# Three edits to a two-layer mixer kernel: layer 0's last pair of chunks, unread matrix products in waits, and the order of one step in the tail

## The chip, the cores and the metric

The kernel runs on one core of a Trainium2 chip. The core has engines that work side by side, each on its own list of instructions, in order: TensorE (PE; its weight loads are shown apart as PEld), VectorE (DVE), ScalarE (ACT), GpSimd (POOL), and SyncE (SP), which issues DMA transfers. The engines wait for each other by semaphores. The metric is the device time of one execution in microseconds, lower is better. The "granted clock" is the share of full speed that TensorE got in a stretch: 1.00 is full, 0.50 half.

## The reference, cut to what matters

The input is an image of 64 x 64 positions with 96 channels. Two layers follow each other; each adds a mixer and an MLP to its input.

```python
# layer 0
x = x + mixer0(ln(x))     # in-projection, depthwise conv, silu, cumulative state sums in 4 directions,
                          # layer norm, times silu(z), out-projection 192 -> 96
t = t + mlp0(ln(t))
# layer 1
x = x + mixer1(ln(x))     # in-projection, dense 3x3 conv over 192 channels, silu,
                          # selective scan in 4 directions, times silu(z), out-projection
t = t + mlp1(ln(t))
```

with

```python
def _layernorm(x, g, b, eps=1e-05):
    m = jnp.mean(x, -1, keepdims=True)
    v = jnp.var(x, -1, keepdims=True)
    return (x - m) * jax.lax.rsqrt(v + eps) * g + b
...
def _qlinear(x, W, b):
    y = q_acc(jnp.einsum('bsk,nk->bsn', q_mul(x), q_mul(W)))
    return q_acc(y + q_mul(b))
```

The MLP is two such linear maps, 96 to 384 and back, with a relu between. `q_mul` rounds to a float of 5 exponent and 2 mantissa bits, `q_acc` to one of 5 and 10 bits; the kernel gets these roundings by writing through fp8 and fp16 tiles.

## The kernel before, in words

The 4096 positions ("tokens") are cut into 8 chunks of 512. The stream `res` stays on the chip, token by token (128 partitions, four tokens each), and products that contract over channels need the chunk turned, channels on partitions; so each norm is followed by four transposes on TensorE and a copy.

The program has these stages: front of layer 0 (to 131 us), back of layer 0 (`back0`, 134 to 255 us), convolution and projections of layer 1 (from 256 us, TensorE alone), the scans (about 490 to 1382 us, VectorE), the tail (1389 to 1461 us).

**The back of layer 0** treats two chunks at a time, in four steps s = 0 to 3, with pairs (0, 2), (1, 3), (4, 6), (5, 7). The loop is skewed: turn s does work of step s + 1 (`centred`, `variance`), of step s, and of step s - 1 (`to_layer1`, `keep_in_proj`). The parts:

- `centred` (L1068): mean over the 192 channels by a product with a constant matrix `mean`, subtracted on VectorE; squares on ScalarE; GpSimd multiplies by the gate.
- `variance` (L1088): sums of squares, three products into one small tile; a root on ScalarE; two small DMAs bring it to tokens; a reciprocal on VectorE gives `factor`. It is a generator: one product runs where `next` is called, the others between the MLP's up products.
- `gated_sums` (L1105): the out-projection, four f32 products for a pair, and copies `ot` on ScalarE.
- `gated_out` (L1118): for one chunk, four transposes, four VectorE operations that scale by `factor` and add to `res`, then the MLP's norm (`norm_chunk` L160, and a cast to bf16 on GpSimd).
- `mlp_turn`, `mlp_up`, `mlp_down` (L1984 to L2027): four transposes `tf`; three bf16 up products with rounding on ScalarE, VectorE and GpSimd; twelve fp8 down products; the sum with `res`. Then `norm_chunk` again, for layer 1.
- `to_layer1` (L1130): transposes `tr` of that norm, a copy `xt`, and a DMA store of it. `keep_in_proj` (L1138): layer 1's first projection, two f32 products of 512 columns for a chunk, each two passes, and their copies into a padded image (`in_proj`, L326; copies on L333). The convolution reads that image.

`keep` fixes the order of the marked instructions on their engine as written; the others are placed by a scheduler.

**The tail** (`tail` L1797) is a pipeline over the 8 chunks, written as a list of steps that each round goes through for chunks of different age: `new` is the youngest, then `mid`, `next_`, `old`, `done`. All its instructions keep the written order. `mixed` (new): out-projection `o` on TensorE (L1831), the sum into `res` (L1833), mean and centring on VectorE. `square` (new): ScalarE. `deviation` (mid): sum on VectorE (L1845), root on ScalarE (L1846). `normed` (mid): reciprocal (L1850) and product (L1852) on VectorE, cast on GpSimd (L1854). `turned` (next_): transposes on TensorE (L1860) and a copy. Then `up`, `rounded`, `relu`, `down`, `brought`, `added` and `finish` of the MLP. A round thus holds VectorE's instructions for `added`, `mixed`, `normed`, `relu` in that order, and those of TensorE for `turned`, `mixed`, `up`, `down`, `up`.

Of the kernel before, what the change touches and what calls it, by code (L numbers as in the profile page):

```python
# [28 lines left out]
F32 = mybir.dt.float32  # L29
# [10 lines left out]
P = 128  # L40
# [8 lines left out]
CH = 512  # L49
# [71 lines left out]
class Net:  # L121
# [897 lines left out]
    def back0(self):  # L1019

        tc = self.tc
        self.xn_d = self.scratch("xn1", [CD, L])
        with ExitStack() as ctx:
            self.tp = ctx.enter_context(tc.tile_pool(name="af0", bufs=3))
            self.lp = ctx.enter_context(tc.tile_pool(name="al0", bufs=2))  # L1030
            self.pa = ctx.enter_context(tc.tile_pool(name="ps_a0", bufs=3, space=PSUM))
            self.po = ctx.enter_context(tc.tile_pool(name="ps_o0", bufs=2, space=PSUM))
            self.ph = ctx.enter_context(tc.tile_pool(name="ps_h0", bufs=2, space=PSUM))
            self.pt = ctx.enter_context(tc.tile_pool(name="ps_t0", bufs=1, space=PSUM))
            self.w_in = self.w_in1
            n = NCH // 2
            self.sq, self.factor, self.xb, self.xn, self.xt, self.hid = {}, {}, {}, {}, {}, {}

            def chunks(s):
                c0 = s // 2 * 4 + s % 2  # L1040
                return (c0, c0 + 2) if 0 <= s < n else ()

            for s in range(-1, n + 1):
                if s + 1 < n:
                    self.centred(s + 1, chunks(s + 1))
                if 0 <= s < n:
                    self.gated_sums(s, chunks(s))
                for k in range(2):
                    for c in chunks(s - 1)[k : k + 1]:
                        self.to_layer1(c)  # L1050
                    for c in chunks(s)[k : k + 1]:
                        self.gated_out(c)
                for c in chunks(s - 1):
                    self.keep_in_proj(c)
                sums = self.variance(s + 1, chunks(s + 1)) if s + 1 < n else iter(())
                next(sums, None)
                for c in chunks(s):
                    self.mlp_turn(0, c)
                    self.mlp_up(0, c, lambda: next(sums, None))
                for _ in sums:  # L1060
                    pass
                for c in chunks(s):
                    self.mlp_down(0, c)
                    self.xn[c] = self.norm_chunk(self.lp, c, self.eps6, F32, f"c{c}")

    def keep(self, instruction):
        self.tc.keep_in_program_order(instruction)
# [740 lines left out]
    def tail(self, ctx, ph, y, out, parts, rest):  # L1808
# [55 lines left out]
        def up(c, m):  # L1864
            a = ph.tile([P, CH], F32, tag="hs", name=f"h1{c}{m}")
            keep(nc.tensor.matmul(a, w1[:, m * P : (m + 1) * P], xt[c], start=True, stop=True))
            hid[c, m] = a

        def rounded(c, m):
            h = tile3(f"h16{m}", c, [P, CH], F16)  # L1870
            keep(nc.scalar.copy(h, hid[c, m]))
            hid[c, m] = h

        def relu(c, m):
            h = hid[c, m]
            if m == 0:
                keep(nc.scalar.activation(h, h, AF.Relu, bias=b1[:, m : m + 1]))
            else:
                keep(nc.vector.tensor_scalar(h, h, b1[:, m : m + 1], 0.0, ALU.add, ALU.max))
            hid[c, m] = tile3(f"h8{m}", c, [P, CH], FP8)  # L1880
            keep(nc.gpsimd.tensor_copy(hid[c, m], h, saturate=False))  # L1881
# [23 lines left out]
        def pick(s):  # L1905
            return order[s] if 0 <= s < NCH else None

        for s in range(-3, NCH + 1):
            new, mid, next_, old, done = (pick(s + d) for d in (3, 2, 1, 0, -1))
            steps = [  # L1910
                (next_, turned),
                (mid, deviation),
                (done, added),
                (new, mixed),
                (next_, lambda c: (up(c, 0), rounded(c, 0), up(c, 1), rounded(c, 1))),
                (mid, normed),
                (done, finish),
                (next_, lambda c: relu(c, 1)),
                (old, down),
                (next_, lambda c: (up(c, 2), rounded(c, 2))),  # L1920
                (new, square),
                (next_, lambda c: (relu(c, 0), relu(c, 2))),
                (old, brought),
            ]
            before, after = rest.get(s + 3, ([], []))
            for f in before:
                f()
            for c, f in steps:
                if c is not None:
                    f(c)  # L1930
            for f in after:
                f()
# [177 lines left out]
```

## Time and profile before

| what | value |
|---|---|
| median of 4 runs | 1454.28 us |
| lowest and highest run | 1445.24 and 1458.40 us |
| profiled execution | 1462.73 us |
| its span (first to last instruction) | 1460.9 us |
| its mean granted clock | 0.845 |
| PE busy | 1165.8 us (80%) |
| DVE busy | 1154.8 us (79%) |
| ACT busy | 910.1 us (62%) |
| POOL busy | 785.4 us (54%) |

The profile is of one execution, and its times count from the start of its span. In a timeline's row stand the start, the time, the engine, the line, the operation, output and inputs with their shapes, how many were joined in the row, and in brackets how long the engine was idle before, with what released it. Buffer numbers are left out of names, so one name can be of several chunks. Ends of matrix products are modelled, so a busy TensorE isn't one at its peak. Other rows used here: the 20 opening products of the program ("warm", L376; f32, 128 x 128) take from 1.74 to 8.91 us.

### The profile page before, as it was taken

Reading aid. Unit: us, or ns where it says so; the run is one execution under the profiler, and the core shown is the slowest. Engines: PE = TensorE matmul, PEld = TensorE weight load, DVE = VectorE, ACT = ScalarE, POOL = GpSimd, SP = SyncE. Lnnn points to the kernel's source line nnn. Section 1 sums busy time; section 2 is a strip of 40 time slices with the busy share of each in tenths; the row PEclk is TensorE's granted clock in tenths of the full one; section 3 lists DMA queues with packets and bytes.
Section 4 is the critical chain, followed back from the end, with each engine's and each line's share of the span. In section 5 each row is a group of like instructions: output and inputs, shape, how many; then the busy total and the mean of one; then the engine's idle time right before and its main releaser. Section 6 shows DMA issues by size and latency. Waiting matters only on the chain. (4 is left out here: it accounts for less than half of the span.)

```text
span 1460.9 us, 12894 instructions
## 1 busy us (share of the span) xinstructions
PE 1165.8 (80%) x3976; PEld 472.3 (32%) x3976; DVE 1154.8 (79%) x887; ACT 910.1 (62%) x1099; POOL 785.4 (54%) x461
## 2 busy tenths in 40 slices
PE   7998776999991787777776777767778888899875
PEld 4532223333430222222222222222223333344343
DVE  6294675023059999999999999999999999999875
ACT  3355564035066677777777776777777777778444
POOL 2001331000006677688877877787878677885445
PEclk7799896999995888888888888888889898978855
DMA  2044000004248453645473456545465547442201
GB/s 64 11 149 100 12 12 22 15 18 110 70 141 256 172 169 112 223 140 171 139 241 115 148 184 195 165 142 183 166 186 156 161 137 252 142 132 86 73 0 44
DMA packets 68850, 183.19 MB, mean 125 GB/s; under 512 B 21488, under 2 KB 35460, under 8 KB 61956
## 3 DMA queue, kind: packets, MB, share of 16 engines
q1 hardware_dynamic: 67480, 182.00, 40.2%
q8 instruction: 33, 0.54, 0.2%
q10 hardware_dynamic: 1292, 0.28, 0.1%
q14 instruction: 45, 0.37, 0.1%
HBM read 155.98 MB, written 20.47 MB: 121 GB/s over the span
## 5 line engine op out<-in xcount | busy, mean ns | idle before, releaser
L1573 POOL TENSOR_TENSOR hss<-h1s,xws 128x1024 f32<-128x1024 f32 x96 | 224.5, 2375 | 135.5 <-PE hs L1581 135.5
L1557 ACT ACTIVATE da<-dt1s,a 128x1024 f32<-128x1024 f32 x168 | 187.9, 1118 | 139.8 <-DVE xws L1568 83.7
L1581 PE MATMUL hs<-hss,ident 128*128 128x512 f32 x376 | 216.3, 659 | 53.1 <-DMA x2s<-bc 32.8
L1568 DVE TENSOR_TENSOR_SCAN xws<-da,xws 128x1024 f32<-128x1024 f32 x96 | 224.1, 2335 | 10.4 <-DVE xws L1568 2.7
L1557 ACT ACTIVATE da<-dt0s,a 128x1024 f32<-128x1024 f32 x168 | 187.4, 1115 | 70.6 <-DVE xws L1568 52.3
L1581 PE MATMUL hs<-h0s,ident 128*128 128x512 f32 x376 | 203.4, 624 | 0.4 <-DVE h0s L1568 0.4
L1568 DVE TENSOR_TENSOR_SCAN h1s<-da,h1s,xws 128x1024 f32<-128x1024 f32 x72 | 169.2, 2350 | 11.0 <-ACT da L1557 2.3
L1581 PEld LDWEIGHTS hs<-hss,ident 128*128 128x128 f32 x376 | 70.6, 204 | 185.9 <-issue 81.8
L1396 POOL TENSOR_TENSOR dun<-u,dtn 128x512 f32<-128x512 f32 x4 | 5.9, 1479 | 197.2 <-DVE dtn L1293 107.6
L1581 PEld LDWEIGHTS hs<-h0s,ident 128*128 128x128 f32 x376 | 76.0, 202 | 100.6 <-issue 95.7
L1602 PE MATMUL acc<-hc2s,fold 128*32 128x512 f32 x128 | 47.5, 832 | 61.3 <-POOL hc2s L1591 58.2
L1602 PE MATMUL acc<-hc0s,fold 128*32 128x512 f32 x128 | 46.8, 819 | 52.8 <-POOL hc0s L1591 52.8
L1602 PE MATMUL acc<-hc1s,fold 128*32 128x512 f32 x128 | 45.5, 799 | 51.1 <-POOL hc1s L1591 51.1
L1541 POOL TENSOR_TENSOR x1s<-x1s,dus 128x1024 f32<-128x1024 f32 x32 | 75.0, 2362 | 8.8 <-DMA x1s<-bc 8.8
L1541 POOL TENSOR_TENSOR x2s<-x2s,dus 128x1024 f32<-128x1024 f32 x32 | 75.1, 2361 | 6.4 <-DMA c1s<-bc 6.4
L1568 DVE TENSOR_TENSOR_SCAN x0s<-da,x0s 128x1024 f32<-128x1024 f32 x32 | 74.7, 2335 | 4.3 <-ACT da L1557 1.9
L1568 DVE TENSOR_TENSOR_SCAN x1s<-da,x1s 128x1024 f32<-128x1024 f32 x32 | 74.7, 2335 | 3.7 <-ACT da L1557 1.2
L1568 DVE TENSOR_TENSOR_SCAN x2s<-da,x2s 128x1024 f32<-128x1024 f32 x32 | 74.7, 2335 | 3.2 <-ACT da L1557 0.6
L1581 PE MATMUL hs<-x0s,ident 128*128 128x512 f32 x128 | 67.4, 609 | 0.2 <-DVE x0s L1568 0.2
L1581 PE MATMUL hs<-x1s,ident 128*128 128x512 f32 x128 | 66.4, 601 | 0.0
L1541 POOL TENSOR_TENSOR x0s<-x0s,dus 128x1024 f32<-128x1024 f32 x28 | 65.7, 2360 | 0.0
L1253 PE MATMUL cv<-pad,cw 128*128 128x512 f32 x144 | 64.3, 598 | 0.0
(346 smaller groups left out, 2370.8 us busy)
## 6 DMA issues: line engine op xcount, KB each, us to landing
c0s<-bc SPq DMA_DIRECT2D x184, 128.0 KB, 2.6
c1s<-bc SPq DMA_DIRECT2D x184, 128.0 KB, 2.6
x2s<-bc SPq DMA_DIRECT2D x32, 512.0 KB, 5.1
x0s<-bc SPq DMA_DIRECT2D x28, 512.0 KB, 3.6
x1s<-bc SPq DMA_DIRECT2D x28, 512.0 KB, 6.5
dus<-du SPq DMA_DIRECT2D x20, 512.0 KB, 5.4
dt1s<-dt SPq DMA_DIRECT2D x40, 256.0 KB, 6.8
dt0s<-dt SPq DMA_DIRECT2D x40, 256.0 KB, 4.7
```

What stands on the lines that cost most here:

```text
L1253: keep(nc.tensor.matmul(t, cw[0][:, tap, 0:P], v, start=tap == 0, stop=False))
L1396: keep(nc.gpsimd.tensor_tensor(dun, u[1][:, m], dtn, ALU.mult))
L1541: keep(nc.gpsimd.tensor_tensor(x, x, du[:, part[j]], ALU.mult))
L1557: keep(nc.scalar.activation(das[i, s], dts[o][:, part[j]], AF.Exp, scale=self.a6[:, g, k : k + 1]))
L1568: keep(nc.vector.tensor_tensor_scan(to, da, x, start, ALU.mult, ALU.add))
L1573: keep(nc.gpsimd.tensor_tensor(cols(hs)[:, w, :], grid(h1)[:, w, :], grid(xw)[:, w, :], ALU.add))
L1581: keep(nc.tensor.matmul(t, self.ident, x[:, chunk(m)], start=x is hs, stop=x is xs[i % 3]))
L1602: keep(nc.tensor.matmul(to, self.fold4, src, start=k == 0, stop=k == NK - 1))
```

## The change

Three edits.

1. A method `awake(products)` puts that many f32 products of 128 x 128 (`mean` times the identity) on TensorE; they write a PSUM tile that nothing reads. It is called in `back0` in turn -1 with 4 (behind the first means, ahead of the first variance), in turn 0 with 6 (behind the first product of the next variance, ahead of the MLP's transposes), in the last turn of a step (s = 3) with 4, and in turn 4 with 10.
2. The last pair. `gated_sums` of step 3 moves up to step 2's end, between the down products of chunk 4 and those of chunk 6. In turn 3 both `gated_out` come first, then the four products, then `to_layer1` of chunk 4, its `keep_in_proj`, and `to_layer1` of chunk 6, whose `keep_in_proj` moves behind the first chunk's up products. In turn 4 each chunk's projection follows its own transposes, where before both transposes came first.
3. In the tail `normed` of `mid` moves from behind the first up products of `next_` to ahead of `mixed` of `new`. On VectorE the reciprocal and the product so come ahead of the residual sum of the younger chunk; the orders on the other engines stay.

```diff
             for s in range(-1, n + 1):
+                last = s == n - 1
                 if s + 1 < n:
                     self.centred(s + 1, chunks(s + 1))
-                if 0 <= s < n:
+                if 0 <= s < n and not last:
                     self.gated_sums(s, chunks(s))
-                for k in range(2):
-                    for c in chunks(s - 1)[k : k + 1]:
+                if s == -1:
+                    self.awake(4)
+                if last:
+                    for c in chunks(s):
+                        self.gated_out(c)
+                    self.awake(4)
+                    for c in chunks(s - 1):
                         self.to_layer1(c)
-                    for c in chunks(s)[k : k + 1]:
-                        self.gated_out(c)
-                for c in chunks(s - 1):
-                    self.keep_in_proj(c)
+                        if c == chunks(s - 1)[0]:
+                            self.keep_in_proj(c)
+                elif s == n:
+                    self.awake(10)
+                    for c in chunks(s - 1):
+                        self.to_layer1(c)
+                        self.keep_in_proj(c)
+                else:
+                    for k in range(2):
+                        for c in chunks(s - 1)[k : k + 1]:
+                            self.to_layer1(c)
+                        for c in chunks(s)[k : k + 1]:
+                            self.gated_out(c)
+                    for c in chunks(s - 1):
+                        self.keep_in_proj(c)
                 sums = self.variance(s + 1, chunks(s + 1)) if s + 1 < n else iter(())
                 next(sums, None)
+                if s == 0:
+                    self.awake(6)
                 for c in chunks(s):
                     self.mlp_turn(0, c)
                     self.mlp_up(0, c, lambda: next(sums, None))
+                    if last and c == chunks(s)[0]:
+                        self.keep_in_proj(chunks(s - 1)[1])
                 for _ in sums:
                     pass
                 for c in chunks(s):
+                    if s == n - 2 and c == chunks(s)[1]:
+                        self.gated_sums(n - 1, chunks(n - 1))
                     self.mlp_down(0, c)
                     self.xn[c] = self.norm_chunk(self.lp, c, self.eps6, F32, f"c{c}")
+
+    def awake(self, products):
+
+        t = self.pa.tile([P, CH], F32, tag="a", name="awake")
+        for _ in range(products):
+            self.keep(self.nc.tensor.matmul(t[:, 0:P], self.mean, self.ident, start=True, stop=True))
...
                 (done, added),
+                (mid, normed),
                 (new, mixed),
                 (next_, lambda c: (up(c, 0), rounded(c, 0), up(c, 1), rounded(c, 1))),
-                (mid, normed),
                 (done, finish),
```

## The prediction

> **What bounds the kernel now.** I read first the slices of the whole span.
>
> ```profile
> PE   7998776999991787777776777767778888899875
> DVE  6294675023059999999999999999999999999875
> PEclk7799896999995888888888888888889898978855
> ```
>
> One slice is 36.5 us. From slice 14 to slice 37 VectorE is at 9: the scans of layer 1, which the change doesn't touch. Ahead of them, in slices 7 to 11, TensorE is at 9: the dense convolution, which can't start before layer 0's back has delivered its last chunk. Behind them is the tail, with no engine at 9. So a microsecond taken from the back (134.4 to 255.3 us) moves the convolution, the scans and the end by as much, and the same is true of one taken from the tail (1389 to 1461). Section 4 of the page covers only the last microseconds and decides nothing here.
>
> Second, the table of busy times by stretch. After the stretch come its length, then PE, PEld, DVE, ACT, POOL, and the granted clock.
>
> ```profile
> 150.00:160.00 10.00, 4.79 (x20) 1.74 (x16) 6.71 (x20) 4.19 (x10) 3.96 (x5) 0.68 0.00 1
> 160.00:170.00 10.00, 8.20 (x39) 2.63 (x39) 2.99 (x7) 6.45 (x12) 3.57 (x6) 0.63 0.01 0
> 190.00:200.00 10.00, 7.96 (x46) 3.29 (x45) 8.33 (x19) 5.23 (x12) 3.31 (x4) 1.00 0.01 0
> 240.00:250.00 10.00, 3.90 (x21) 2.73 (x22) 7.08 (x15) 3.27 (x8) 1.06 (x2) 0.50 0.06 19
> 260.00:300.00 40.00, 40.00 (x186) 15.35 (x184) 1.41 (x2) 1.26 (x2) 0.00 (x0) 1.00 0.06 14
> ```
>
> No engine fills the back: it is a chain through all of them. In two places its TensorE work runs at half clock, around 160 and from 225 to 252.7 us. 260 to 300 shows the convolution: PE alone, full clock.
>
> Third, TensorE's timeline at those places (start, duration, engine, line, operation, count, idle before and its releaser).
>
> ```profile
> 202.82 3.63 PE L331 MATMUL in<-xt,w_in 96*128 96x512 f32 x8
> 225.55 6.92 PE L331 MATMUL in<-xt,w_in 96*128 96x512 f32 x8
> 246.75 1.06 PE L188 MATMUL tr<-ident,lnxnc 128*96 128x128 f32 x4 [4.38 <-DVE lnxnc L180]
> 249.37 5.23 PE L331 MATMUL in<-xt,w_in 96*128 96x512 f32 x8
> ```
>
> The same eight passes of layer 1's input projection cost 3.63 us in step 2, 6.92 in step 3 and 5.23 in step 4. Only the clock differs. The third row has 4.38 us of idle TensorE, waiting for the last norm.
>
> Fourth, the tail's timeline, one round.
>
> ```profile
> 1424.12 0.30 ACT L1846 ACTIVATE lnvt<-lnvt,columns 128x4 f32<-128x4 f32 x1
> 1425.39 0.56 DVE L1833 TENSOR_TENSOR res<-res,o 128x384 f32<-128x384 f32 x1 [0.93 <-PE o L1831]
> 1427.05 0.17 DVE L1850 RECIPROCAL lnrt<-lnvt 128x4 f32<-128x4 f32 x1
> 1427.32 0.56 DVE L1852 TENSOR_TENSOR lnxqt<-lnxct,lnrt 128x384 fp8e5<-128x384 f32 x1
> 1428.01 0.51 POOL L1854 CAST xbt<-lnxqt 128x384 bf16<-128x384 fp8e5 x1 [2.51 <-DVE lnxqt L1852]
> 1428.57 0.66 PE L1860 MATMUL tf<-identb,xbt 128*96 128x128 bf16 x4 [0.86 <-POOL xbt L1854]
> ```
>
> The root of the older chunk is done at 1424.42, but its reciprocal stands in VectorE's queue behind a residual sum that waits for TensorE, so it runs at 1427.05. Through it TensorE, which has the sum's product behind the transposes, waits 0.86 us: a loop.
>
> [...] in the back the clock changes at 140.0, 153.7, 167.3, 225.3, 232.2, 235.6 and 252.7 us, all multiples of 3.41 us apart within 0.05. [...] the window 150.25 to 153.66 had TensorE busy 1.85 us of 3.41, and the clock fell. [...] the window 221.93 to 225.34 has 1.82 us busy, all transposes, and the clock fell behind it. [...]
>
> **The change part by part.**
>
> *Price of an added product.* The 20 opening products of the program (f32, 128x128, two passes each: 40 passes) take 7.17 us: passes start 0.21 us apart until 6.9 us, where the clock rises, and 0.11 apart after it. So a product costs 0.43 us at half clock, 0.22 at full; 4, 6, 10 cost 1.7, 2.6, 4.3 or 0.9, 1.3, 2.2.
>
> *Four ahead of the first step.* TensorE waits 1.54 us before 141.71, at full clock; 0.9 fits. Cost nothing, gain nothing; if that cover went, 0.9.
>
> *Six ahead of step 0's turn.* TensorE waits 2.98 us for GpSimd's cast until 157.99, at half clock; 2.6 fits by 0.4. [...] The MLP of step 0 (first transpose to last product) takes 11.58 us, from 157.99 to 169.57; in steps 1 and 2, at full clock, 9.52. So the clock is worth 2.06 us here. Both ends: 0 (the clock rises at 167.3 as now) to 2.06. I take half, 1.0.
>
> *Last pair's sums earlier, projections split, four products.* Work is the same plus four products (0.9 to 1.7 us, some 0.5 to 1 on the path, since TensorE's idle time of 1.76 us ahead of 222.04 is filled by the moved transposes). The moved gated sums (3.1 us of TensorE) lie between step 2's down products, which wait 1.12 us for GpSimd; their two copies on ScalarE (0.58 each) then stand ahead of the copy of chunk 6's down product there, and GpSimd's cast of chunk 7's norm comes behind two casts of hidden tiles. SyncE's stores of the transposed chunks go along with the transposes; nothing in the back waits for them (cost nothing; one store, 3 us, if something did). The four products need one of three PSUM tiles that the projections use, free at that point; the same holds for the ten. I laid all instructions from step 2's down products to the last copy into the padded image in the new order, each engine in order, with the trace's durations. With the clock as it was granted before: 0 us gained. At full clock before and after: 0.9 us lost. At half clock throughout: 1.2 lost. So the reordering in itself brings nothing (0 to −1.2); its use is that transposes no longer stand alone for a window. New order at full clock against before as granted: 5.1 us gained, with the next edit's share in it.
>
> *Ten in front of the last two chunks.* They lie in the 4.38 us gap. At full clock 2.2, at half 4.3: it just fits. With 1.0 us of down products just ahead, TensorE is then busy about 5.3 us, and holds a whole window of 3.41 in some 55% of positions. What it is worth: transposes 1.06 to 0.61 twice, projections 5.23 to 3.63, less what VectorE's norm at 248.2 gates: up to 1.8 us, within the 5.1.
>
> *Sum for the back.* The windows stand where they happen to stand against the program, so the clock's gain is between 0 and 5.1 + 2.1 = 7.2. I take half of 5.1 and half of 2.1, 3.5 together, less 0.5 for the products that lie on the path: **3.0 us**.
>
> *The tail.* Reciprocal and product, 0.17 + 0.56 us, leave the loop: after them the cast could end at about 1425.7, and TensorE's transposes follow its own last product, at about 1427.7 instead of 1428.57. That is up to 0.86 us in each of four rounds, 3.4. Against it: after the swap VectorE waits for ScalarE's root in the early rounds, where the reciprocal stood under the sum (0.4 us once, its wait in the last round: 1443.72 + 0.30 to 1444.06); one round is held by gating of an earlier quarter (1.56 us before 1430.79); and the end is a chain of copies on ScalarE and casts on GpSimd, with 2.7 us waits that don't shrink. Both ends: −0.4 to +2.5. I take **1.5 us**. Nothing moves on TensorE, ScalarE, GpSimd or SyncE there.
>
> Profiled execution: 1462.73 us, of which 1460.9 span; 4.5 less is about 1458.2. It lies 8.45 us (0.6%) above the median of the runs, 1454.28, which themselves spread over 13 us. The difference carries over to the median: **1449.8**.
>
> **The rivals.**
> 1. *Clock lifted only in parts*, the forecast: 1449.8, chance 0.50.
> 2. *Clock full from step 0 on* to the end of the back (7.2) and the tail's best (2.5): 1444.6, chance 0.17. For it: steps 1 and 2 stay full with TensorE 75 to 80% busy. Against: windows with half of it already fell.
> 3. *The clock doesn't rise*, the products only fill waits: back 0, tail 1.5: 1452.8, chance 0.20. For it: the window 225.34 to 228.76 was full by the records and the clock rose only after the next. Then the change doesn't do what it says.
> 4. *Slower: the unread products run at half clock on the path.* TensorE can't pass them: ten at 4.3 us started 0.5 late, plus four at 1.7, plus the reordering's 1.2, with 2.6 us of six. On the path 0.5 + 1.2 + 0.5 + 1.2 = 3.4 us; and the tail gains nothing as VectorE stands before the root. 1457.7, chance 0.13. It decides from the point where the ten products end after the norm's product for the next to last chunk (246.6 us in the trace of before).
>
> **How the numbers follow.** About 1%, 14.5 us, is what a measurement of this kernel can tell from no change (four runs spread 13). Every case lies within it. The scatter of a median adds some 3 us to each case. The range 1443 to 1457.5 holds the first three with that scatter, and leaves out the lower part of case 2 and half of case 4. Faster by over 1%: 0.05, from case 2 and scatter; slower by over 1%: 0.03; within: 0.92.
>
> **What would show it.** Granted clock over 0.75 in the stretches that answer to 150 to 170 and 225 to 250; the projections in steps 3 and 4 near 3.6 us rather than 6.9 and 5.2; the start of the convolution (255.8) near 252.8; tail rounds from sum to sum below 5.98 us. Wrong if unread products delay the transposes behind them, if the reciprocal shows waits for the root of over 0.5 us in every round, or if the scans' length changes.

## The result, and the profile after

The changed kernel takes 1445.07 us (median of 39 runs, 1438.28 to 1454.53). The kernel before, run beside it, takes 1450.96 us (60 runs, 1443.99 to 1462.66). The ratio is 0.9955, with a 95% interval of 0.9939 to 0.9971: by the ratio 6.5 us faster, at least 4.2 and at most 8.9. Forecast were 4.5 us less, to 1449.8, from a median of four runs that lay 3.3 us above that of sixty.

The profiled execution of the changed kernel has a span of 1443.3 us, 17.6 less than the one of before. That is far more than 6.5, so the first question to the two traces is where the 17.6 lie. I cut both at the same instructions: the first product with `mean` (start of the back), the first `spread4p` (start of the convolution), the first out-projection `o` (start of the tail), the last instruction. "Half" is the time at half clock in the stage, the program's opening left out.

| us | front (half) | back (half) | convolution, scans | tail | span |
|---|---|---|---|---|---|
| before | 134.4 (39) | 121.1 (43) | 1133.9 | 71.6 | 1460.9 |
| changed | 124.9 (14) | 116.8 (27) | 1131.8 | 69.8 | 1443.3 |
| difference | -9.5 | -4.3 | -2.0 | -1.7 | -17.6 |

The largest difference is in the front, whose code is the same in both. The experiments deal with it; the back and the tail sum to 6.0.

The 2.0 us in the scans, whose code is the same too, aren't chance. VectorE's timeline at one place of the scans, before, and below it changed:

```profile
574.19 2.29 DVE L1568 TENSOR_TENSOR_SCAN xws<-da,xws 128x1024 f32<-128x1024 f32 x1
576.94 7.25 DVE L1568 TENSOR_TENSOR_SCAN xws<-da,xws 128x1024 f32<-128x1024 f32 x3 [0.46 <-DVE xws L1568]
```

```profile
560.47 9.65 DVE L1597 TENSOR_TENSOR_SCAN xws<-da,xws 128x1024 f32<-128x1024 f32 x4
```

Before, VectorE is idle for 0.46 us ahead of the second scan; in the changed kernel the same four scans follow each other. From the start of the first to that of the second it takes 2.75 us before and 2.39 changed. This is so at six places, every 64 scans: 2.1 us. All four kernels below with the old order in the back (before, tail_only, awake_only, front_hold) have 2.75 at all six, and all ten with the new order 2.39 or 2.40, with unread products or without. VectorE's instructions and their order are the same. So this gain goes with the second edit, whose code stands far from it. Why the idle time is there is open: the trace names VectorE's own scan before, which had ended at 576.48.

The slices of the span, after:

```profile
PE   7998778999981776787776777677779888899875
DVE  6494683033169999999999999999999999999876
PEclk8999997999995889888888888888889899987855
```

The scans fill VectorE as before. The clock's row differs in the first slices (7799 before, 8999 now): that is the front.

Busy times by stretch of the changed kernel (length, PE, PEld, DVE, ACT, POOL, granted clock, DMA share, GB/s); its back lies at 124.9 to 241.7 us:

```profile
140.00:150.00 10.00, 7.26 (x32) 3.78 (x32) 6.19 (x19) 4.73 (x11) 3.34 (x4) 0.83 0.00 1
150.00:160.00 10.00, 6.96 (x39) 3.20 (x38) 5.86 (x13) 5.60 (x11) 3.94 (x6) 0.83 0.01 0
220.00:230.00 10.00, 7.65 (x37) 4.06 (x36) 5.14 (x8) 4.83 (x10) 4.47 (x7) 0.50 0.01 0
230.00:240.00 10.00, 8.66 (x35) 6.28 (x34) 5.51 (x12) 3.64 (x9) 0.00 (x0) 0.76 0.12 32
```

Step 0's MLP (147 to 157) now has 0.83 where it had 0.63 to 0.68, and the last chunks (230 to 240) 0.76 where they had 0.50. The last MLP (220 to 230) is still at half clock.

TensorE's timeline in the last two turns:

```profile
211.05 1.98 PE L331 MATMUL in<-xt,w_in 96*128 96x512 f32 x4 [0.67 <-ACT xt L189]
214.02 0.61 PE L188 MATMUL tr<-ident,lnxnc 128*96 128x128 f32 x4 [0.99 <-DVE lnxnc L180]
216.63 0.42 PE L188 MATMUL tf<-identb,xb 128*96 128x128 bf16 x4 [2.00 <-POOL xb L2010]
219.42 3.62 PE L331 MATMUL in<-xt,w_in 96*128 96x512 f32 x4
229.50 4.60 PE L1093 MATMUL awake<-ident,mean 128*128 128x128 f32 x20
234.08 0.95 PE L188 MATMUL tr<-ident,lnxnc 128*96 128x128 f32 x4
235.71 1.98 PE L331 MATMUL in<-xt,w_in 96*128 96x512 f32 x4 [0.67 <-ACT xt L189]
238.80 1.98 PE L331 MATMUL in<-xt,w_in 96*128 96x512 f32 x4 [0.67 <-ACT xt L189]
```

Four passes cost 1.98 us at full clock and 3.62 at half. The clock falls at 217.7, behind 3.41 us in which TensorE had 0.73 us of transposes and otherwise waited, 2.0 us of it in one piece. It is back at 234.8, 17.06 us or five times 3.41 later. In this trace too, all changes of the clock lie multiples of 3.41 us apart; "window" is used below for such a stretch, with its edges where the clock's changes in the same trace put them. The ten products take 4.60 us, and the transposes follow without a wait: they start 4.66 us after the start of the last down product, exactly as before, where TensorE stood idle for 4.38 us. (Below, stretches "from the last down product" count from its start.)

The tail, one of the changed kernel's later rounds:

```profile
1403.15 0.18 DVE L1879 RECIPROCAL lnrt<-lnvt 128x4 f32<-128x4 f32 x1 [1.57 <-ACT lnvt L1875]
1403.43 0.56 DVE L1881 TENSOR_TENSOR lnxqt<-lnxct,lnrt 128x384 fp8e5<-128x384 f32 x1
1404.13 0.51 POOL L1883 CAST xbt<-lnxqt 128x384 bf16<-128x384 fp8e5 x1 [2.07 <-DVE lnxqt L1881]
1404.46 0.55 DVE L1862 TENSOR_TENSOR res<-res,o 128x384 f32<-128x384 f32 x1 [0.46 <-PE o L1860]
1406.57 0.63 PE L1889 MATMUL tf<-identb,xbt 128*96 128x128 bf16 x4
```

The product comes before the residual sum, though its reciprocal waited 1.57 us for ScalarE's root, the cast is done at 1404.64, and the transposes at 1406.57 wait for nothing. From out-projection to out-projection this round takes 4.89 us; the round in its place took 5.98.

### The profile page after: what moved, and what is told of

It is laid out like the page before. It is cut to its first block, busy times and chain, and to the rows that moved or that the text cites. A ratio compares the mean times of both kernels' runs of the same rounds, so it can differ in the third digit from the quotient of the medians.

```text
span 1443.3 us, 12990 instructions
## 1 busy us (share of the span) xinstructions
PE 1154.0 (80%) x4024; PEld 472.0 (33%) x4024; DVE 1156.2 (80%) x887; ACT 909.9 (63%) x1099; POOL 785.1 (54%) x461
## 5 line engine op out<-in xcount | busy, mean ns | idle before, releaser
L1602 POOL TENSOR_TENSOR hss<-h1s,xws 128x1024 f32<-128x1024 f32 x96 | 224.6, 2377 | 134.4 <-PE hs L1610 134.4
L1610 PE MATMUL hs<-h0s,ident 128*128 128x512 f32 x376 | 199.6, 613 | 0.8 <-DVE h0s L1597 0.8
```

The lines of the kernel that those rows point to most:

```text
L1602: keep(nc.gpsimd.tensor_tensor(cols(hs)[:, w, :], grid(h1)[:, w, :], grid(xw)[:, w, :], ALU.add))
L1610: keep(nc.tensor.matmul(t, self.ident, x[:, chunk(m)], start=x is hs, stop=x is xs[i % 3]))
```

## The experiments

All stages, cut as above, with mean and standard deviation of the runs and the ratio to the kernel before that ran beside them:

| kernel | front (half) | back (half) | conv., scans | tail | mean (s.d., runs) | ratio (95%) |
|---|---|---|---|---|---|---|
| before | 134.4 (39) | 121.1 (43) | 1133.9 | 71.6 | 1452.1 (5.2, 60) | 1 |
| changed | 124.9 (14) | 116.8 (27) | 1131.8 | 69.8 | 1445.6 (5.1, 39) | 0.9955 (0.9939 to 0.9971) |
| tail_only | 119.1 (0) | 121.7 (38) | 1133.3 | 70.2 | 1451.5 (5.4, 20) | 0.9991 (0.9963 to 1.0018) |
| back_only | 126.1 (17) | 116.8 (27) | 1133.0 | 71.2 | 1448.1 (4.5, 20) | 0.9967 (0.9943 to 0.9990) |
| order_only | 127.8 (21) | 120.0 (38) | 1133.0 | 71.2 | 1452.7 (4.4, 12) | 1.0010 (0.9979 to 1.0041) |
| awake_only | 130.5 (27) | 120.3 (34) | 1131.4 | 71.6 | 1449.3 (5.6, 12) | 0.9969 (0.9930 to 1.0007) |
| doubled | 121.5 (7) | 120.0 (24) | 1129.1 | 71.2 | 1446.2 (3.2, 20) | 0.9954 (0.9935 to 0.9973) |
| no_ten | 119.1 (0) | 120.7 (35) | 1135.5 | 71.2 | 1453.7 (4.9, 20) | 1.0010 (0.9988 to 1.0032) |
| hold | 121.6 (7) | 114.3 (17) | 1132.8 | 70.2 | 1443.8 (4.3, 20) | 0.9937 (0.9918 to 0.9956) |
| hold_late | 133.4 (35) | 115.4 (19) | 1132.7 | 69.2 | 1442.9 (5.3, 17) | 0.9941 (0.9917 to 0.9965) |
| front_hold | 118.9 (2) | 124.1 (50) | 1133.9 | 71.6 | 1448.0 (2.1, 22) | 0.9962 (0.9943 to 0.9981) |
| all_hold | 119.2 (2) | 115.2 (19) | 1132.6 | 69.2 | 1438.1 (1.3, 7) | 0.9898 (0.9863 to 0.9933) |
| tail_awake | 119.2 (1) | 116.7 (20) | 1132.2 | 77.3 | 1445.9 (1.9, 20) | 0.9954 (0.9935 to 0.9972) |
| change_front | 118.9 (2) | 117.2 (26) | 1130.7 | 69.8 | 1439.3 (1.8, 6) | 0.9912 (0.9881 to 0.9943) |

### The change taken apart: tail_only and back_only

```diff
 # tail_only: the kernel before, and only
+                (mid, normed),
                 (new, mixed),
...
-                (mid, normed),
```

> The tail's edit alone. My theory (reciprocal and product leave the loop between TensorE and VectorE): the tail, from its first out-projection to the end, takes 69.8 us as in the changed kernel and not 71.6; rounds 5 and 7 take 4.9 instead of 6.0; the back stays at 117 to 123, wherever the clock's windows fall; total 1.7 us less, ratio 0.9988. Rival (the tail was only shorter by a different granted clock): tail 71.6, ratio 1.000.

By time it can't be told from no change (0.9991, 1 within the interval). By the trace it can: the tail takes 70.2 us, and 71.2 to 71.6 in all seven kernels with the old order of tail and without further edits there. Rounds 5 and 7 take 4.89 and 4.86 us. The half-clock time in the tail is 65.6 of 70.2 us, where before has 68.2 of 71.6, so the gain isn't the clock's.

`back_only` is the changed kernel with the tail's step `normed` back in its old place.

> The back's edits alone (last pair and unread products), tail as before. My theory: back 114 to 119 us against 121 before, tail 71.6, ratio 0.9967 (4.8 us less). Rival (most of the gain is the tail's or chance): back 120 or more, ratio 0.999 or more.

The back takes 116.8, the tail 71.2, the ratio is 0.9967: as expected. The two parts add up, to 0.9958 against 0.9955 for the whole.

### Order or clock: order_only and awake_only

```diff
 # order_only: back_only without its four calls
-                    self.awake(4)
...
-                    self.awake(10)
...
-                if s == 0:
-                    self.awake(6)
```

> Only the last pair's new order, without any unread product, tail as before. My theory (the order gains nothing by itself, only the clock does): step 3 and 4 together, from step 2's last down product to the convolution, stay within 1.2 us of before when the clock is granted alike; ratio 0.999 to 1.001. Rival (the order is what gains, as the projections no longer stand in one block ahead of the MLP's transposes): back 117 us, ratio 0.997.

From step 1's last down product to the convolution order_only takes 62.7 us, and the kernels with the old order 61.9 (before), 62.6 (tail_only) and 65.0 (front_hold, where the clock fell once more in between). The changed kernel takes 59.7. The ratio, 1.0010 (0.9979 to 1.0041), shows no gain, though the 2.1 us of the scans, which this kernel has as well, would fit into its interval. That the back is 1.1 shorter than before's lies ahead of the last pair, in code that this kernel doesn't change. So in the back the order by itself gains nothing, as I had reckoned. back_only differs from it in the products alone, and ran beside it: 116.8 against 120.0 us in the back, 27 against 38 of them at half clock, and means of 1448.1 against 1452.7 us. This is the plainest sign that the products, by the clock, are what gains.

```diff
 # awake_only: the kernel before, with the products in the same waits
+                if s == -1:
+                    self.awake(4)
+                if s == n:
+                    self.awake(10)
                 for k in range(2):
+                    if s == n - 1 and k == 0:
+                        self.awake(4)
                     for c in chunks(s - 1)[k : k + 1]:
                         self.to_layer1(c)
...
                 next(sums, None)
+                if s == 0:
+                    self.awake(6)
...
```

> Only the unread products (4, 6, 4, 10, in the same turns and waits), order and tail as before. My theory (the clock gains): step 0's MLP 9.6 us instead of 11.4, last down product to convolution 12 instead of 13.4, half-clock time in the back 20 to 30 us instead of 43; back 117 to 119, ratio 0.997 to 0.998. Rival (unread products on the path): back 122 to 124, ratio 1.001.

Half a miss. From the last down product to the convolution it takes 11.2 us, against 13.4 before: the ten work in the old order too. But step 0's MLP, from its first transpose, took 11.1 us, as the clock was at half from 154.7 to 161.5, in the middle of it. And in step 3 the clock was at half ahead of the four products and again behind them (16.3 us from step 2's last down product to step 3's transposes, against 15.0 before; front_hold, without any products there, has 16.4). Back 120.3. The ratio, 0.9969 with 1 in the interval, tells little.

### How much the ten are worth, and what twice as many cost: no_ten and doubled

`no_ten` is back_only without the call with 10.

> Back's edits without the ten products ahead of the last two chunks, tail as before. My theory (the ten lift the clock for the last transposes and projections): from step 3's last down product to the convolution 14.0 to 14.6 us instead of 12.1; back 118.8 to 119.3; ratio 0.998. Rival (the ten only fill the wait): 12.1 to 12.5 there, back 117.

TensorE's timeline of no_ten at the end of the back:

```profile
228.06 1.06 PE L188 MATMUL tr<-ident,lnxnc 128*96 128x128 f32 x4 [4.38 <-DVE lnxnc L180]
229.79 3.78 PE L331 MATMUL in<-xt,w_in 96*128 96x512 f32 x4 [0.67 <-ACT xt L189]
235.10 3.78 PE L331 MATMUL in<-xt,w_in 96*128 96x512 f32 x4 [0.67 <-ACT xt L189]
```

The 4.38 us wait is back, and every pass behind it is at half clock: 16.4 us from the last down product to the convolution, where back_only has 12.1, more even than the 14.0 to 14.6 that I expected. How much more differed with the place of the windows: order_only, which lacks the ten too, has 14.6, and there the clock rose 3.6 us ahead of the convolution, and in no_ten only 5.6 us into it. So in no_ten the convolution begins at half clock and takes 2.7 us more to the first scan (196.7 against 194.0). Ratio 1.0010: without the ten, no gain is left that the runs show.

```diff
 # doubled: back_only with
-                    self.awake(4)
+                    self.awake(8)
...
-                    self.awake(4)
+                    self.awake(8)
...
-                    self.awake(10)
+                    self.awake(20)
...
-                    self.awake(6)
+                    self.awake(12)
```

> Back's edits with twice the unread products (8, 12, 8, 20), tail as before. In the changed kernel's trace the ten end just when the norm's product for the next transposes comes (both waits from the last down product to the transposes are 4.66 us). If a product costs 0.43 us at half clock, ten more put about 4.3 us on the path ahead of the last two chunks when the clock is half, and 2.2 when it is full; six more 1.3 to 2.6 less what is left of step 0's wait (0.5): back 120 to 124 us against 116.8 with the single number, ratio to before 0.999 to 1.002. Rival (more products hold the clock at full, so that the projections and the transposes win it back): back 114 to 117, ratio 0.995 to 0.997.

```profile
227.84 6.62 PE L1093 MATMUL awake<-ident,mean 128*128 128x128 f32 x40
234.29 0.60 PE L188 MATMUL tr<-ident,lnxnc 128*96 128x128 f32 x4
```

TensorE's timeline: the twenty take 6.62 us, half of them at full clock, and the transposes come 6.5 us after the last down product instead of 4.7. The stretch to step 0's transposes, with the eight and the twelve in it, takes 0.8 more, the one to step 3's transposes 1.3 more. In the profile the back takes 120.0 us, 3.3 more than with the single number, as my theory had it: from the point where the wait is full, each product is on the path. The ratio is the rival's, though: 0.9954, where I expected 0.999 or more and back_only has 0.9967 (the intervals overlap). So the runs don't show that twice as many are slower; only the trace does. In the profile the convolution and the scans took 1129.1 us, 4 less than back_only's. Those stages have the same code in both, and range from 1129.1 to 1135.5 over all kernels. Of that range no_ten's 2.7 us and the 2.1 that go with the back's order are located; doubled has the latter too. 2.0 of its 4 lie between the last scan and the tail (5.5 us against 7.5), as in awake_only; why is open.

### Two waits that were left: hold and hold_late

```diff
 # hold: the changed kernel with
...
                     for c in chunks(s - 1):
                         self.to_layer1(c)
+                    for c in chunks(s - 1):
                         self.keep_in_proj(c)
...
                 if s == 0:
                     self.awake(6)
+                if last:
+                    self.awake(8)
```

> The changed kernel with two more edits in the back: eight unread products in TensorE's 2.0 us wait ahead of the last pair's first MLP transposes, where the changed kernel's clock falls (217.7 us), and turn 4 in the old order (both transposes, then both projections). My theory: the clock doesn't fall in the last turn, so from step 2's last down product to step 3's last is 20.5 us instead of 23.0; the last stretch to the convolution 11.2 instead of 12.2; back 113 to 114, tail 69.8, ratio 0.993. Rival (the window is decided by more than that wait, and the products delay the cast's readers): 23 to 24 us there, back 116, ratio 0.995.

TensorE's timeline of hold, where the changed kernel had its clock fall:

```profile
211.22 1.95 PE L1096 MATMUL awake<-ident,mean 128*128 128x128 f32 x16
213.39 0.42 PE L188 MATMUL tf<-identb,xb 128*96 128x128 bf16 x4 [0.22 <-POOL xb L2013]
215.81 1.88 PE L331 MATMUL in<-xt,w_in 96*128 96x512 f32 x4
```

The eight fit into the wait, with 0.22 us left of it. The clock stays at full until 221.6. Step 2's last down product to step 3's last takes 21.5 us (23.0), the last stretch 11.2 (12.2), the back 114.3, ratio 0.9937; the interval overlaps the changed kernel's, so that the runs don't separate the two.

```diff
 # hold_late: hold, with
-                (mid, normed),
+                (None if s == -2 else mid, normed),
                 (new, mixed),
                 (next_, ...),
+                (mid if s == -2 else None, normed),
```

> As hold, with the tail's new order left out in its second round alone, where the norm's product is held by GpSimd's long product (1.85 us instead of 0.56) and holds the residual sum behind it. My theory: the tail's second round takes 6.6 us instead of 8.3, and the tail 68.5 instead of 69.8, ratio 0.992. Rival (a later round is held by a gate of its own and takes the gain back): tail 69.8, with a longer third or fourth round.

What it is about is the changed kernel's second round in the tail (timeline):

```profile
1379.93 2.34 POOL L1620 TENSOR_TENSOR hc1s<-hc1s,dus 128x1024 f32<-128x1024 f32 x1 [3.31 <-PE o L1860]
1380.63 0.18 DVE L1879 RECIPROCAL lnrt<-lnvt 128x4 f32<-128x4 f32 x1 [0.36 <-ACT lnvt L1875]
1380.84 1.85 DVE L1881 TENSOR_TENSOR lnxqt<-lnxct,lnrt 128x384 fp8e5<-128x384 f32 x1
1382.61 0.54 DVE L1862 TENSOR_TENSOR res<-res,o 128x384 f32<-128x384 f32 x1
```

The norm's product takes 1.85 us instead of 0.56, and ends 0.42 us behind GpSimd's product; the residual sum behind it, whose operands have been ready, comes late. In the old order this round took 6.55 us, in the new one 8.28. But the round ahead of it was shorter, 4.20 against 4.97, and it is so in awake_only and doubled too, which have the old order: the two rounds have to be summed. Together they took 11.5 before and 12.5 changed, 1.0 more. In hold_late they take 11.5 again, and 12.5 in hold. The tail follows: 69.2 us in hold_late and 70.2 in hold. (In the changed kernel, with 69.8, the end comes 23.5 us behind the last out-projection, in hold 23.9, though the code of the tail is the same.) That is half a miss, as I expected 68.5 for the tail, and the ratio (0.9941) doesn't separate it from hold.

### The front: front_hold, all_hold, change_front

The front has one code in all kernels and took 119 to 134 us, by its time at half clock. In eight of the first ten profiles the clock fell at 17 to 20 us and came back only at 24 to 55. TensorE's timeline of before, and below it of no_ten, one of the two where it didn't fall:

```profile
17.30 1.06 PE L409 MATMUL tr<-ident,lnxna 128*96 128x128 f32 x4 [1.98 <-DVE lnxna L405]
```

```profile
17.47 0.61 PE L409 MATMUL tr<-ident,lnxna 128*96 128x128 f32 x4 [2.16 <-DVE lnxna L405]
```

Both have the wait of 2 us; what differs in the traces is how the windows lie over it. In before, an edge between two windows is at 17.1: the window that ends there has TensorE busy for 1.61 of 3.41 us, with products, not transposes. In no_ten the edge is at 16.7 and divides the wait, and the windows on both sides are busy for 1.98 and 1.93 us. In the other eight it was alike: in tail_only, with 1.98 and 2.09, the clock stayed at full, and in seven it fell behind windows with 0.75 to 1.82 us.

```diff
 # front_hold: the kernel before, with
+            if i == 3:
+                warm = pm.tile([P, CH], F32, tag="m", name="warm3")
+                for _ in range(8):
+                    keep(nc.tensor.matmul(warm[:, 0:P], self.ident, self.ident, start=True, stop=True))
             if mid is not None:
```

> The kernel before, with eight unread products in one wait of the front, before the transposes of chunk 2 (TensorE waits 2.0 to 2.2 us there for VectorE's norm, and in eight of ten profiles the clock fell just after it, at 17 to 20 us, and stayed at half until 24 to 55 us). My theory (the scatter of the runs is this one drop: the front takes 119.1 us where it doesn't happen and 121 to 134 where it does): front 119 to 120 us, half-clock time in it 0 besides the opening, ratio 0.994 to 0.996, and the runs lie closer together than the 18 us of the kernel before. Rival (the scatter is in the scans): front as before on average, 126, ratio 0.999 to 1.001, same scatter.

```profile
15.13 1.95 PE L394 MATMUL warm<-ident 128*128 128x128 f32 x16
17.30 0.61 PE L413 MATMUL tr<-ident,lnxna 128*96 128x128 f32 x4 [0.22 <-DVE lnxna L409]
```

The front takes 118.9 us, the clock stays at full but for 2 us, the ratio is 0.9962, and the standard deviation of the runs falls from 5.1 to 2.1 us. So most of the scatter of the kernel before is this one wait. The profiled execution of before, with 134.4 us in the front, was a bad draw: the mean of the first ten profiles is 125.8.

`all_hold` has hold_late's edits and front_hold's.

> The changed kernel with all that the runs point to: eight products in the front's wait, eight in the wait of the last pair, old order in turn 4, and the tail's old order in its second round. If the parts add: front 119.5, back 114.3, tail 69.2, against 126 (mean of the profiles), 121 and 71.4 of before: 15.8 us less, ratio 0.989. Rival (the front's clock and the back's are tied by the same windows, so that one gain takes from the other): 0.992 or more.

1438.18 us median, ratio 0.9898 where 0.989 was expected if the parts add, standard deviation 1.3: the best of all, faster than both the kernel before and the changed one. The rival's 0.992 still lies within the interval (0.9863 to 0.9933).

`change_front` is the changed kernel with front_hold's lines.

> The changed kernel with the same eight products in the front's wait as front_hold, so that the change can be measured without the front's scatter: front_hold has a mean of 1447.97 us and a standard deviation of 2.1. If the change is worth what the stages of the profiles sum to (back 5.5, tail 1.3), the mean is 1441.2, ratio to the kernel before 0.992, standard deviation about 2. If only the predicted 4.5 are there: 1443.5. Rival (part of the measured 6.5 us is the front's chance): 1445 or more.

Its mean is 1439.3, front_hold's 1448.0: 8.6 us for the change without the front's scatter. The two ran on different chips; by their ratios (0.9912 and 0.9962) it is 7.3, and by the intervals of both 2 to 12.5. The stages give back 5.3, tail 1.3 and scans 2.1, together 8.7. The rival's 1445 lies outside what the ratio allows (at most 1443.8, from the 1452.1 of before): there is a gain of the change itself. How much it is above the forecast 4.5 these six runs leave open.

### The same means in the tail: tail_awake

```diff
 # tail_awake: all_hold with, ahead of each round's steps (awake as above, identity times identity)
+            if -3 < s < NCH - 1:
+                awake(8)
```

> all_hold with eight more unread products at the head of each of the tail's rounds 2 to 9, where the granted clock is half for 66 of 69 us. Theory A (the same means lifts the clock here): the tail's rounds are then held by ScalarE at 4.4 us, tail 64 to 67 us. Theory B ([...] the unread products stand on the path at 0.43 us each): eight rounds with up to 3.4 us each, tail 75 to 90 us. I hold B somewhat likelier.

Busy times by stretch, of all_hold and below it of tail_awake:

```profile
1400.00:1410.00 10.00, 7.21 (x37) 5.65 (x37) 8.60 (x17) 5.81 (x13) 5.95 (x9) 0.50 0.05 20
```

```profile
1400.00:1410.00 10.00, 9.89 (x57) 8.89 (x57) 4.25 (x9) 4.48 (x10) 3.62 (x5) 0.73 0.06 21
```

Each theory has half of it. The clock is lifted for more than half of the time (30 us at half instead of 66), as A had it. But TensorE is now full, with the unread products on the path, and the tail takes 77.3 us instead of 69.2, as B had it; the ratio is 0.9954, where all_hold has 0.9898. In these runs the means pays where TensorE waits for longer than the products take (hold, 1.95 us of products and 0.22 of the wait left), and not in this loop, which TensorE itself closes.

## Why the prediction was right, point by point

- **Sign and size.** 4.5 us were forecast, 6.5 measured. Back and tail, the two places named, gain, and the clock is what gains in the back (back_only against order_only). The range of 1443 to 1457.5 shows little, since the kernel before lies in it too. The gain shows more: of the four cases, 9.7, 4.5 and 1.5 us faster and 3.4 slower, only 4.5 lies within 4.2 to 8.9. There is luck in the size all the same: the clock's share was half of a span from 0 to 7.2 (2.55 and 1.05, written as 3.5, are 3.6), the back gave more than it, and the scans gave something that wasn't in the sum.
- **The scans, named as untouched.** Wrong, and one of the prediction's own signs of being wrong came true: their length changes. From the first scan to the end of the last it is 933.6 us before and 931.2 changed, and 2.1 of that goes with the back's order. (They begin at 448.6 us, slice 12 of the first view counted from 0, not 14; nothing rests on that.)
- **Price of a product.** Right, but for 0.2 to 0.3 us in which the last one ends: four took 1.08 us at full clock (0.9 forecast), ten 4.60 at half (4.3).
- **Four ahead of the first step: nothing.** Right: they end in the wait, 0.46 us of it left, and the stretch to step 0's transposes is 22.3 to 23.6 us with them and 22.5 to 23.6 without.
- **Six in step 0: 1.0.** Nearly right, by a longer way. Step 0's MLP, to the start of its last product, takes 9.3 to 11.1 us in the nine kernels with six (mean 9.95) and 10.9 to 11.8 in the four without (11.2). But the stretch behind it, to step 1's transposes, is 15.5 instead of 15.0 on average, since the clock now mostly falls behind step 0's down products, where it had just risen before. 0.8 is left, of means whose ranges overlap.
- **The last pair's order alone: 0 to -1.2.** Right in the back (order_only); the scans' 2.1 us go with it.
- **The ten: up to 1.8, and half of 5.1 for all of the last pair.** This is the term that was mis-sized. Up to the convolution back_only is 2.5 us ahead of order_only and 4.3 ahead of no_ten, and of the latter by another 2.7 in it. I had compared with the old order, where the clock rose at 252.7 us, behind a window that the projections' own eight passes filled (3.41 of 3.41 us); in the new order the passes alternate with transposes, and without the ten the clock rose later against the convolution, 3.6 us ahead of it in one trace and 5.6 us into it in the other. Old order and ten together (awake_only, hold) are best, 11.2 us. For the back as a whole: 121.1, 121.7 and 124.1 without the back's edits, 116.8, 116.8 and 117.2 with them, 5.3 us on average against 3.0 forecast.
- **The tail: 1.5.** Its size is right (1.3: 71.2 to 71.6 without, 69.8 to 70.2 with the edit), and its sum was not. I had up to 0.86 us in each of four rounds; two, the fifth and the seventh, gain 1.1 each. What I charged against it, waits for ScalarE's root, is 0.36 us in three of the eight rounds and 1.57 in a fourth, the one shown above, which gains all the same. What I didn't charge is the norm's product beside GpSimd's, 1.85 us instead of 0.56, and so 1.0 us over the first two rounds.
- **Rivals.** Clock full throughout (1444.6): the measured median, 1445.07, is almost its number, but that is mostly the 3.3 us by which the four runs of before lay too high; 27 us of the back are still at half, and four of the last pair's projection passes still take 3.62 us. Clock not lifted (1452.8): not this, the granted clock in step 0's MLP is 0.83. Slower, products on the path (1457.7): its turning point was where the ten end after the norm's product; that ends at 233.9 and they at 234.1, so the kernel stands at the edge, and doubled's trace shows the other side, 3.3 us.
- **What I passed over.** I took the 8.45 us between the profiled execution and the median as something to carry over. They were mostly the front's half-clock time, as its 134.4 us against a mean of 125.8 suggest. It is visible in the clock's row (7799) and larger than the whole change.

## What to carry to other kernels

A TensorE wait of 2 us can cost many microseconds behind it: the clock that fell there stayed at half in before from 17.1 to 54.7 us, and the front took 134.4 us where front_hold's took 118.9. Eight unread products in that wait (1.95 us) kept it at full; as many as fit and no more, since doubled's twenty took 6.62 us and its back 3.3 us more. Cut two traces at the same instructions before comparing them: a stage with unchanged code tells what chance does, here in the front over twice the change. But compare several kernels before calling it chance: the scans' 2.1 us look like noise in one pair of traces, and divide fourteen without an exception. An instruction moved up on one engine should be looked at for what the other engines run in its new place.

## What the runs showed of the hardware

- **The clock fell at waits of 2 us.** In the front of before TensorE waits 1.98 us, and the clock fell at 17.1 us, behind a window with 1.61 us of products; in the changed kernel's last turn it waits 2.00 us, and the clock fell at 217.7 us, behind one with 0.73 us of transposes. With eight products in the same waits, 1.95 us, it stayed at full (front_hold, hold). In the traces of before and changed together the clock fell ten times ahead of the convolution, behind windows with TensorE busy for 0.71 to 1.99 of 3.41 us; but it stayed at full behind six others with 1.73 to 1.99. (The ends of matrix products are modelled, so these sums are rough by some hundredths.) In the changed kernel's tail it stayed at half though TensorE was busy without a break from 1402.15 to 1408.98 us. So what decides, and which products count, isn't shown.
- **The scatter of a kernel's runs can be the clock's.** Front 118.9 to 119.2 us without the fall, 121 to 134 with it; standard deviation of the runs 5.1 and 2.1 us.
- **VectorE's product took longer beside GpSimd's.** In the changed kernel's tail the norm's product takes 1.85 us in the second round and 2.16 in the fourth, where GpSimd's product of 2.34 us began before it; both times it ends 0.42 us behind that one. In the other six rounds it takes 0.56 to 0.75. The residual sum, one of whose inputs is in PSUM, took 0.55 us beside GpSimd's product at 1375.6 us. Why the one was longer and the other not isn't shown.
